# Feeding an adjacency copy into a graph-attention kernel piece by piece, and spreading softmax denominators earlier than they are used

## Chip, cores and metric

One Trainium2 chip, one core. The time is device microseconds of one launch. The kernel before takes 3400.32 us, the median of three runs (3393.2 to 3400.7); the profiled execution spans 3398.4 us. In what follows PE is the matrix engine, DVE the vector engine, ACT the scalar engine, POOL the general engine (it also issues one of the DMA queues), SP the engine that issues the other main DMA queue.

## What is computed

Two graph layers on 4096 nodes with 512 features and one 4096 x 4096 zero/one adjacency. Cut to what matters:

```python
# layer 0: layernorm + relu, then an attention auto-encoder, 4 heads of 128 features
Xw  = einsum('hnd,hde->hne', Xh, W)
sig = sigmoid(f1[:, :, None] + f2[:, None, :])
att = masked_softmax(adj * sig, adj != 0)       # the same att for encoder and decoder
Xa  = einsum('hij,hjd->hid', att, Xw)           # encoder attention
emb = mlp_block(batchnorm(Xa))                  # 512 x 512 product, elu, residual, batchnorm
Y   = einsum('hij,hjd->hid', att, emb)          # decoder attention
out = mlp_block(elu(Y @ W^T));  x = x + out
# layer 1: layernorm + relu, graph attention (GAT), 4 heads of 128
logits = leaky_relu(e_s[:, :, None] + e_n[:, None, :]) + (-1e10) * (1 - adj)
x = x + relu(softmax(logits) @ feats + b)
```

So three attentions of 4 heads x 4096 x 4096 weights each, all float32, with a softmax denominator per target node.

## The kernel before, in words

**Stages.** A first stage normalises x, transposes it and computes the projected features (loop over eight node blocks `ib` of 512, L432-480). Then come encoder attention, an MLP, decoder attention, an MLP, the GAT projection (L695-724) and GAT attention. Features are kept transposed in SBUF: [128 features, 4096 nodes] for each head.

**One attention block.** `attention` (L201) runs eight blocks `n`, one per head `h` and half `tb` of the targets (TB = 2048 targets). A block has 32 steps `j`, each for 128 source nodes. A step loads a mask tile `a` (128 x 2048 bytes, L198, five buffers), makes a weight tile `e` [128, 2048] (encoder and decoder: two ACT passes L400, L401 and the mask multiply on DVE L402; GAT: one ACT pass L761 and one DVE instruction L762) and multiplies it into four PSUM banks with four products of 512 columns (L332, in the profile two records each). The decoder reads every fifth weight tile back from DRAM, where the encoder stored it (`ekeep`).

**Denominators.** They need the sum of all 32 weight tiles over the 128 sources. Each tile goes one of three ways, by the lists ENC_FIRST (encoder blocks 0 and 1), ENC and GAT (L62-64): *moved* tiles are added up in DRAM (`dacc`, L344, a POOL-issued DMA that accumulates, the first of a block only writes; read back at j = 30, L302); *by ones* tiles are multiplied with a matrix of ones on PE (L286); all others are added on DVE into `acc` (L350 the first pair, L352 the rest). At the end PE sums `acc` and the tile read back into the bank `den`.

**Ending of a block.** It is done inside the next block (`ending`, L256), by the list `later` that `at(j, ...)` fills. At step EVICT = 2 ACT copies `den` out (L235), POOL stores it to DRAM (`dens`, L236) and reads it back spread over the partitions (`dcol`, L238); the four output slices are taken out of PSUM. At step 5 DVE inverts (L242, L243) and POOL stores `rinvs` (L244). At steps 6, 9, 12, 15 `spread` (L246) loads slice s of the inverses to all 128 partitions (`rb`, two buffers, L249, POOL queue); at steps 8, 11, 14, 17 DVE scales the slice by it (L491 encoder and decoder, L770 GAT) and two steps later comes the second finishing step (statistics L494, or elu L603, or relu and the output L773, L779).

**What sets the order.** Each engine runs its own list in order. The lists are made by the framework from the program: among the instructions it takes to be ready it prefers the earlier one in the program, so a program position is a preference and not a fixed place. `tc.issue_after(x)` only keeps instructions of x's engine behind x. Everything that POOL issues by DMA (`dacc`, `dens`, `dcol`, `rinvs`, `rb`, the adjacency copy) goes to one DMA queue; mask tiles and x go to SP's; `ekeep` stores to ACT's.

**The adjacency copy.** The input adjacency is float32 in DRAM. Eight DMAs on POOL's queue (L428) copy it as bytes into `masks[t][g]` (t the half of the targets, g a quarter of the sources; 8 MB read and 2 MB written each). Mask tiles are loaded from these. All eight are issued in a row, each made to wait for the last load of x.

Of the kernel before, what the change touches and what calls it, by code (L numbers as in the profile page):

```python
# [41 lines left out]
NIB = N // IB  # L42
# [17 lines left out]


ENC_FIRST = (), (4, 5, 10, 11, 15, 16, 20, 21, 25, 26, 30, 31)  # L62
ENC = (2, 5, 8, 11, 14, 17, 20, 23, 26), (3, 4, 12, 13, 30, 31)
GAT = (1, 3, 6, 8, 11, 13, 16, 18, 21, 23, 26), (14, 30, 31)

KEEP = 5

# [12 lines left out]
def kernel(ctx, tc, x, xT, adjT, w0, w0T, v0, wencT, wdecT, vecs, w1, w1T, a1, outT):  # L80
# [120 lines left out]
    def attention(what, keep, pools, weights, values, row_of, out, finish, ebufs, modes=None, invert=None,  # L201
# [54 lines left out]
        def ending(h, tb, po, den):  # L256

            dcol = denominators(h, tb, den) if den is not None else None
            outs = [out(spool, h, tb, s, po[s]) for s in range(SB)]
            if dcol is not None:  # L260
                at(EVICT + 3, invert_them, h, tb, dcol)
            rbs = {}
            for s, o in enumerate(outs):
                at(EVICT + 4 + 3 * s, lambda s=s: rbs.update({s: spread(h, tb, s)}))
                for k, f in enumerate(finish):
                    at(EVICT + 6 + 3 * s + 2 * k, lambda f=f, s=s, o=o: f(spool, h, tb, s, o, rbs[s], False))

        def next_row_of(h, tb):
            rowb = keep.tile([P, TB], FP, name="rowb", bufs=2)
# [6 lines left out]
        for n, (h, tb) in enumerate(blocks):  # L276
# [15 lines left out]
            for j in range(NJ):  # L292
                for f in later.pop(j, []):
                    f()
                with tc.issue_after(a_load.ins) if j else nullcontext():
                    if (n, j) in extras:
                        extras[n, j]()
                    if not last and j == NJ - 10:
                        next_row = next_row_of(*blocks[n + 1])
                if moved and j == NJ - 2:  # L300
                    back = weight_tile()
                    nc.gpsimd.dma_start(back, dacc[tb])  # L302
                e = weight_tile()
                store = j % KEEP == KEEP - 1 and kept is not None
                if store and kept == "read":
                    a_load = nc.sync.dma_start(e, ekeep[h][tb][j // KEEP])
                else:
                    if masks0:
                        a, a_load = masks0.pop(0)
                    else:  # L310
                        a = mask_tile(keep)
                        a_load = load_mask(a, tb, j)
                    weights(e, rowb, a, j, h, SB if n + j == 0 else 1)
                    if store:
                        stores.append((j // KEEP, e))

                    if j % KEEP == KEEP - 3 and stores:
                        k, t = stores.pop()
                        nc.scalar.dma_start(ekeep[h][tb][k], t)

                def products():
                    nonlocal last_main, last_ones

                    with tc.issue_after(last_ones.ins) if last_ones is not None else nullcontext():

                        if j == EVICT:
                            po.append(bank())
                            for k, t in ahead:
                                nc.tensor.matmul(po[-1], block(values[h], k), t[:, (SB - 1) * IB:SB * IB],
                                                 start=(k == 0), stop=False)  # L330
                        for s, b in enumerate(po):
                            last_main = nc.tensor.matmul(b, block(values[h], j), e[:, s * IB:(s + 1) * IB],  # L332
                                                         start=(j == 0), stop=(j == NJ - 1))
                    last_ones = None


                early = last and j == NJ - 1 and invert is not None
                if not early:
                    products()
                if j < EVICT:  # L340
                    ahead.append((j, e))
                if invert is not None:
                    if j in moved:
                        nc.gpsimd.dma_start(dacc[tb], e, **({"accum_op": ALU.add} if j > moved[0] else {}))  # L344
                    elif j in by_ones:
                        held.append(e)
                    else:
                        adds.append(e)
                        if len(adds) == 2:
                            nc.vector.tensor_add(acc, *adds)  # L350
                        elif len(adds) > 2:
                            nc.vector.tensor_add(acc, acc, e)  # L352

                    if held and j + 1 not in by_ones:
                        with tc.issue_after(last_main.ins):
                            for t in held:
                                add_to_den(t)
# [48 lines left out]
    with tc.tile_pool(name="keep", bufs=1) as keep:  # L406

        with tc.tile_pool(name="f_small", bufs=1) as small, tc.tile_pool(name="f_work", bufs=2) as work:
            xs, loads = [], []
            w0x = small.tile([P, H, DX], FP, name="w0x")  # L410
            v0s = small.tile([P, H, 2], FP, name="v0s")
            nc.scalar.dma_start(v0s, v0)
# [1 line left out]
            for ib in range(NIB):  # L414
                if ib < NIB - 3:
                    xs.append(small.tile([P, C, F], FP, name=f"xs{ib}"))
                else:
                    xs.append((w, *(R[4][:, k * C * F:(k + 1) * C * F].rearrange("p (c f) -> p c f", f=F)
                                    for k in range(2)))[ib - NIB + 3])
                xin = x[ib * IB:(ib + 1) * IB, :].rearrange("(c p) f -> p c f", p=P)  # L420

                for c in range(0, C, 1 if ib == 0 else C):
                    n = 1 if ib == 0 else C
                    loads.append(nc.sync.dma_start(xs[ib][:, c:c + n, :], xin[:, c:c + n, :]))

            for t in range(NTB):
                for g in range(NJ // MG):
                    cast = nc.gpsimd.dma_start(masks[t][g], adjT[g * MG * P:(g + 1) * MG * P, t * TB:(t + 1) * TB])  # L428
                    tc.add_manual_dep(cast.ins, loads[-1].ins.name,
                                      mybir.DependencyInfo(mybir.DependencyClass.Sync, mybir.DependencyReason.DATA),  # L430
                                      reason="features first")
            for ib in range(NIB):  # L432
                st = work.tile([P, C, 6], FP, name="st")
                mv = work.tile([P, C, 2], FP, name="mv")
# [7 lines left out]
                for c in range(C):  # L442
                    by_pool = c == C - 1
                    hn = work.tile([P, F], FP, name="hn", tag="hnp" if by_pool else "hn")
                    (nc.gpsimd if by_pool else nc.vector).tensor_scalar(
                        hn, xs[ib][:, c, :], mv[:, c, 0:1], rstd[:, c:c + 1], ALU.subtract, ALU.mult)
                    pt = bank().rearrange("p (f n) -> p f n", n=P)
                    for fb in range(C):
                        last_pe = nc.tensor.transpose(pt[:, fb, :], hn[:, fb * P:(fb + 1) * P], ident)
                    last_act = nc.scalar.activation(hT[:, :, c * P:(c + 1) * P], pt, AF.Relu)  # L450
# [45 lines left out]
        def encoder_weights():  # L496
            nc.sync.dma_start(w, wencT.rearrange("(c p) o -> p c o", p=P))


# [10 lines left out]
        def three_heads():  # L510
            bn_coefs(stats, "enc_bn_gamma", "enc_bn_beta", a_att, b_att, 0, C - 1)
            add_to_bias(bank(), 0, C - 1, vec_of("enc_mlp_b"))
            for fb in range(C - 1):
                scale_weights(fb)

        with tc.tile_pool(name="enc", bufs=1) as spool:

            with tc.issue_after(last_act.ins), tc.issue_after(masks0[-1][1].ins):
                attention("enc", keep, spool, tanh_weights, R[0:4], lambda h, tb: (rows[tb], h), out_enc,
                          (scaled, statistics), 7, lambda n: ENC if n > 1 else ENC_FIRST, (TINY, ALU.max), "write",  # L520
                          row0=row0, masks0=masks0,
                          extras={(2, 8): encoder_weights, (H * NTB - 1, NJ // 2): three_heads})


        def mlp_block(work, w, src, dst, gamma, beta, scale, between, early=None):
# [255 lines left out]
    with tc.tile_pool(name="gat", bufs=1) as spool:  # L781
        x1_last = []

        def load_last():
# [48 lines left out]
```

## Time and profile before

| stage | us, about | what is busy there |
|---|---|---|
| first stage, and start of encoder block 0 | 0 to 79 | PE, DVE, ACT in turn |
| encoder block 0 | 79 to 209 | ACT 120.5 of 130 |
| encoder block 1 up to the inversion | 209 to 246 | PE 11.1, DVE 9.2, ACT 19.1 of 37 |
| rest of encoder block 1 | 246 to 372 | PE 120.7, ACT 102.9, DVE 116.3 of 126 |
| encoder blocks 2 to 7 | 372 to 1120 | PE 117 to 121, ACT 111 to 119 of 124 or 125 each |
| MLP | 1116 to 1275 | PE 155.1 of 159 |
| decoder attention | 1275 to 2162 | PE 884.5 of 887 |
| MLP's end and GAT projection | 2162 to 2425 | PE 247.5 of 263 |
| GAT attention, 8 blocks | 2425 to 3398 | PE 107 to 124, DVE 100 to 123, of 118 to 130 each |

Read it row by row and not by the page's averages: PE is busy 96% of the span over all, so what can still be won lies in the few places where it is not. The span of a block is the distance between two first denominator additions (L350) on DVE.

### The profile page before, as it was taken

Reading aid. Unit: us, or ns where it says so; the run is one execution under the profiler, and the core shown is the slowest. Engines: PE = TensorE matmul, PEld = TensorE weight load, DVE = VectorE, ACT = ScalarE, POOL = GpSimd, SP = SyncE. Lnnn points to the kernel's source line nnn. Section 1 sums busy time; section 2 is a strip of 40 time slices with the busy share of each in tenths; the row PEclk is TensorE's granted clock in tenths of the full one; section 3 lists DMA queues with packets and bytes.
Section 4 is the critical chain, followed back from the end, with each engine's and each line's share of the span. In section 5 each row is a group of like instructions: output and inputs, shape, how many; then the busy total and the mean of one; then the engine's idle time right before and its main releaser. Section 6 shows DMA issues by size and latency. Waiting matters only on the chain.

```text
span 3398.4 us, 26074 instructions
## 1 busy us (share of the span) xinstructions
PE 3255.4 (96%) x8943; PEld 1501.3 (44%) x8943; DVE 2679.7 (79%) x1912; ACT 2598.4 (76%) x1908; POOL 325.5 (10%) x479
## 2 busy tenths in 40 slices
PE   7969999999999999999999999989999999999999
PEld 6423344344344464444444444448544344444443
DVE  6969799899898775665666556585699999999998
ACT  7969799999999438999999999565665564656553
POOL 2000000010010000000000000024201111111110
PEclk9989999999999999999999999989999999999999
DMA  9994578778777103434444344231388788788876
GB/s 190 195 158 146 163 225 241 205 214 240 208 227 200 55 13 136 142 130 138 145 141 136 133 139 139 62 127 69 94 206 205 186 216 192 196 207 201 208 187 169
DMA packets 180309, 559.60 MB, mean 165 GB/s; under 512 B 20372, under 2 KB 23700, under 8 KB 144208
## 3 DMA queue, kind: packets, MB, share of 16 engines
q0 software_dynamic: 43232, 211.14, 31.7%
q1 hardware_dynamic: 126288, 293.66, 25.8%
q10 hardware_dynamic: 10656, 53.15, 3.9%
q8 instruction: 70, 1.15, 0.1%
q14 instruction: 63, 0.52, 0.0%
HBM read 391.78 MB, written 233.19 MB: 184 GB/s over the span
## 4 chain that ended last, share of the span: by engine, by line
PE 57%; DVE 19%; DMA 11%; issue 9%; ACT 3%; POOL 1%; DVEq 0%; ACTq 0%; POOLq 0%
PE ps L332 42%; DVE e L762 7%; PE ps L533 6%; DMA a<-mask 5%; DVE R L352 5%; DVE e L402 4%; PE ps L707 3%; DMA rb<-rinvs 3%; DMA rinvs<-dcol 1%; PE den L286 1%; DVE acc L352 1%; ACT e L401 1%; ACT e L400 1%; PE ps L467 1%; PE ps L588 1%
## 5 line engine op out<-in xcount | busy, mean ns | idle before, releaser
L332 PE MATMUL ps<-e,R 128*128 128x512 f32 x6048 | 2661.4, 601 | 104.3 <-DVE e L402 70.9
L332 PEld LDWEIGHTS ps<-e,R 128*128 128x128 f32 x6048 | 1155.8, 192 | 1600.2 <-issue 1437.4
L402 DVE TENSOR_TENSOR e<-e,a 128x2048 f32<-128x2048 f32 (+1 forms) x470 | 1050.2, 2259 | 372.5 <-ACT e L401 348.3
L400 ACT ACTIVATE e<-rowb,score 128x2048 f32<-128x2048 f32 (+1 forms) x470 | 913.5, 1968 | 82.4 <-PE ps L332 46.6
L401 ACT ACTIVATE e<-e 128x2048 f32<-128x2048 f32 (+1 forms) x470 | 872.8, 1882 | 44.1 <-DVE e L402 37.6
L761 ACT ACTIVATE e<-rowb,nq,jcol 128x2048 f32<-128x2048 f32 x224 | 454.6, 2085 | 206.9 <-DMA dacc<-e 165.0
L762 DVE SCALAR_TENSOR_TENSOR e<-e,jcol,a 128x2048 f32<-128x2048 f32 (+1 forms) x259 | 589.7, 2316 | 3.8 <-DMA a<-mask 2.6
L352 DVE TENSOR_TENSOR R<-R,e 128x2048 f32<-128x2048 f32 x128 | 291.5, 2278 | 0.0
L352 DVE TENSOR_TENSOR acc<-acc,e 128x2048 f32<-128x2048 f32 x126 | 288.1, 2287 | 2.2
L344 POOL DMA_DIRECT2D dacc<-e x142 | 117.8, 830 | 1087.9 <-DMA dacc<-e 432.7
L533 PE MATMUL ps<-R,w 128*128 128x512 f32 x512 | 220.3, 592 | 0.6 <-DVE w L501 0.6
L249 POOL DMA_DIRECT2D rb<-rinvs x88 | 47.9, 547 | 1135.4 <-DVE R L491 874.5
L533 PEld LDWEIGHTS ps<-R,w 128*128 128x128 f32 x512 | 97.2, 190 | 122.7 <-issue 117.9
L773 ACT ACTIVATE R<-R,vec 128x512 f32<-128x512 f32 x32 | 23.1, 722 | 142.2 <-DVE R L770 141.7
L707 PE MATMUL ps<-w1x,hT 128*128 128x260 f32 x512 | 117.5, 388 | 2.8 <-ACT hT L683 2.8
L553 ACT ACTIVATE ex<-ps,bias 128x512 f32<-128x512 f32 x64 | 44.1, 688 | 97.5 <-PE ps L533 80.4
L707 PEld LDWEIGHTS ps<-w1x,hT 128*128 128x128 f32 x512 | 97.7, 193 | 22.8 <-ACT hT L683 4.4
L286 PE MATMUL den<-e,ones 128*32 128x512 f32 x784 | 93.6, 598 | 0.0
L761 ACT ACTIVATE e<-w,nq,jcol 128x2048 f32<-128x2048 f32 (+1 forms) x35 | 65.6, 1938 | 35.7 <-DMA dacc<-e 32.4
L491 DVE TENSOR_TENSOR R<-R,rb 128x512 f32<-128x512 f32 x60 | 40.5, 686 | 51.6 <-DMA rb<-rinvs 39.4
L555 DVE SCALAR_TENSOR_TENSOR ex<-ex,re 128x512 f32<-128x512 f32 x64 | 45.0, 703 | 36.2 <-ACT re L554 36.1
L712 ACT ACTIVATE R<-ps,rstd 128x128 f32<-128x128 f32 x128 | 38.6, 368 | 39.8 <-PE ps L707 38.9
(154 smaller groups left out, 1209.1 us busy)
## 6 DMA issues: line engine op xcount, KB each, us to landing
a<-mask SPq DMA_DIRECT2D x720, 256.0 KB, 3.3
dacc<-e POOLq DMA_DIRECT2D x142, 1024.0 KB, 8.6
ekeep<-e ACTq DMA_DIRECT2D x48, 1024.0 KB, 9.4
e<-ekeep SPq DMA_DIRECT2D x48, 1024.0 KB, 4.9
rb<-rinvs POOLq DMA_DIRECT2D x88, 256.0 KB, 3.8
mask<-in_adjT POOLq DMA_DIRECT2D x8, 2048.0 KB, 117.6
rowb<-rows SPq DMA_DIRECT2D x16, 1024.0 KB, 6.7
e<-dacc POOLq DMA_DIRECT2D x14, 1024.0 KB, 5.3
```

Of the source, the lines that this page charges most:

```text
L249: nc.gpsimd.dma_start(rb, everywhere(rinvs[h][tb], 0, s * IB, IB))
L286: last_ones = nc.tensor.matmul(den[s * 32:(s + 1) * 32, :], ones[:, 0:32], t[:, s * IB:(s + 1) * IB], start=not begun, stop=stop)
L332: last_main = nc.tensor.matmul(b, block(values[h], j), e[:, s * IB:(s + 1) * IB], start=(j == 0), stop=(j == NJ - 1))
L344: nc.gpsimd.dma_start(dacc[tb], e, **({"accum_op": ALU.add} if j > moved[0] else {}))
L352: nc.vector.tensor_add(acc, acc, e)
L400: nc.scalar.activation(e, rowb, AF.Tanh, bias=column(score[:, 1], j, h), scale=0.5)
L401: nc.scalar.activation(e, e, AF.Exp, scale=0.5)
L402: nc.vector.tensor_mul(e, e, a)
L533: nc.tensor.matmul(z, w[:, fb, o * P:(o + 1) * P], nodes(src[fb], ib), start=(fb == 0), stop=(fb == C - 1))
L707: nc.tensor.matmul(b[:, 0:2 * DX], hT[:, fb, c * P:(c + 1) * P], w1x[:, fb, 2 * k:2 * k + 2, :].rearrange("p h x -> p (h x)"), start=(fb = ...
L761: nc.scalar.activation(e, rowb, AF.Relu, bias=column(nq, j, h), scale=column(jcol, j, h))
L762: nc.vector.scalar_tensor_tensor(e, e, column(jcol2, j, h), a, ALU.add, ALU.mult)
```

## The change

Three edits. The lists ENC and GAT are moved: as many tiles go each way as before (9 moved and 6 by ones; 11 moved and 3 by ones), but the first moved tile is now the block's first, and the others come a step or two earlier (GAT, ENC) or, for by-ones tiles, elsewhere. The ending of a block inverts at step 7 instead of 5, spreads at steps 8, 9, 14, 15 instead of 6, 9, 12, 15, and uses each spread slice five steps after it is issued instead of two; the second finishing step follows one step later instead of two. And the adjacency copy is issued one piece at a time: piece n behind POOL's part of the normalisation of node block n + 1, waiting for the first half of x instead of all of it; the eighth piece is issued in encoder block 1 at step 12. It is for the denominators' DMAs to wait less behind other transfers and for the engines to wait less for them.

```diff
-ENC = (2, 5, 8, 11, 14, 17, 20, 23, 26), (3, 4, 12, 13, 30, 31)
-GAT = (1, 3, 6, 8, 11, 13, 16, 18, 21, 23, 26), (14, 30, 31)
+ENC = (0, 3, 6, 9, 12, 15, 18, 21, 24), (4, 5, 13, 14, 30, 31)
+GAT = (0, 2, 5, 7, 10, 12, 15, 17, 20, 22, 25), (9, 30, 31)
...
-                at(EVICT + 3, invert_them, h, tb, dcol)
+                at(EVICT + 5, invert_them, h, tb, dcol)
             rbs = {}
             for s, o in enumerate(outs):
-                at(EVICT + 4 + 3 * s, lambda s=s: rbs.update({s: spread(h, tb, s)}))
+                j = EVICT + 6 + s % 2 + s // 2 * 6
+                at(j, lambda s=s: rbs.update({s: spread(h, tb, s)}))
                 for k, f in enumerate(finish):
-                    at(EVICT + 6 + 3 * s + 2 * k, lambda f=f, s=s, o=o: f(spool, h, tb, s, o, rbs[s], False))
+                    at(j + 5 + k, lambda f=f, s=s, o=o: f(spool, h, tb, s, o, rbs[s], False))
...
-            for t in range(NTB):
-                for g in range(NJ // MG):
-                    cast = nc.gpsimd.dma_start(masks[t][g], adjT[g * MG * P:(g + 1) * MG * P, t * TB:(t + 1) * TB])
-                    tc.add_manual_dep(cast.ins, loads[-1].ins.name, ...)
+                if ib == NIB // 2 - 1:
+                    half_loaded = load
+            def copy_adjacency(n, behind):
+                t, g = divmod(n, NJ // MG)
+                cast = nc.gpsimd.dma_start(masks[t][g], adjT[g * MG * P:(g + 1) * MG * P, t * TB:(t + 1) * TB])
+                tc.add_manual_dep(cast.ins, behind.ins.name, ...)
...
+                    if by_pool and ib > 0:
+                        with tc.issue_after(made.ins):
+                            copy_adjacency(ib - 1, half_loaded)
...
+                          extras={(1, 12): lambda load: copy_adjacency(7, load),
```

More of the change, by code (lines that the diff above doesn't have):

```diff
@@ L296, in attention @@
                     if (n, j) in extras:
-                        extras[n, j]()
+                        extras[n, j](a_load)
                     if not last and j == NJ - 10:
@@ L408 @@
         with tc.tile_pool(name="f_small", bufs=1) as small, tc.tile_pool(name="f_work", bufs=2) as work:
-            xs, loads = [], []
+            xs = []
             w0x = small.tile([P, H, DX], FP, name="w0x")
@@ L423 @@
                     n = 1 if ib == 0 else C
-                    loads.append(nc.sync.dma_start(xs[ib][:, c:c + n, :], xin[:, c:c + n, :]))
-            for t in range(NTB):
-                for g in range(NJ // MG):
-                    cast = nc.gpsimd.dma_start(masks[t][g], adjT[g * MG * P:(g + 1) * MG * P, t * TB:(t + 1) * TB])
-                    tc.add_manual_dep(cast.ins, loads[-1].ins.name,
-                                      mybir.DependencyInfo(mybir.DependencyClass.Sync, mybir.DependencyReason.DATA),
-                                      reason="features first")
+                    load = nc.sync.dma_start(xs[ib][:, c:c + n, :], xin[:, c:c + n, :])
+                if ib == NIB // 2 - 1:
[3 more added lines that the diff above has]
+                cast = nc.gpsimd.dma_start(masks[t][g], adjT[g * MG * P:(g + 1) * MG * P, t * TB:(t + 1) * TB])
+                tc.add_manual_dep(cast.ins, behind.ins.name,
+                                  mybir.DependencyInfo(mybir.DependencyClass.Sync, mybir.DependencyReason.DATA),
+                                  reason="others first")
             for ib in range(NIB):
@@ L444 @@
                     hn = work.tile([P, F], FP, name="hn", tag="hnp" if by_pool else "hn")
-                    (nc.gpsimd if by_pool else nc.vector).tensor_scalar(
+                    made = (nc.gpsimd if by_pool else nc.vector).tensor_scalar(
                         hn, xs[ib][:, c, :], mv[:, c, 0:1], rstd[:, c:c + 1], ALU.subtract, ALU.mult)
+                    if by_pool and ib > 0:
+                        with tc.issue_after(made.ins):
+                            copy_adjacency(ib - 1, half_loaded)
                     pt = bank().rearrange("p (f n) -> p f n", n=P)
@@ L494, in statistics, with encoder_weights @@
             nc.vector.bn_stats(stats[:, h, tb * SB + s, :], o)
-        def encoder_weights():
+        def encoder_weights(load):
             nc.sync.dma_start(w, wencT.rearrange("(c p) o -> p c o", p=P))
@@ L508, in add_to_bias, with three_heads @@
             nc.vector.tensor_add(bias, pb[:, 0:C], base)
-        def three_heads():
+        def three_heads(load):
             bn_coefs(stats, "enc_bn_gamma", "enc_bn_beta", a_att, b_att, 0, C - 1)
@@ L521 @@
                           row0=row0, masks0=masks0,
[L522 removed]
+                          extras={(1, 12): lambda load: copy_adjacency(7, load),
+                                  (2, 8): encoder_weights, (H * NTB - 1, NJ // 2): three_heads})
         def mlp_block(work, w, src, dst, gamma, beta, scale, between, early=None):
@@ L782, with load_last @@
         x1_last = []
-        def load_last():
+        def load_last(load):
             x1_last.append(spool.tile([P, TB], FP, name="rowb", bufs=2))
```

## The prediction

> **What bounds the kernel now.** I read the page first, then the table of windows by stage, then who waits for whom in the stages where an engine is short of work, then the landing times of single transfers. The windows of encoder block 1's start, an encoder block, the decoder and a GAT block (stretch, length, then busy time of PE, weight loads, DVE, ACT, POOL, PE clock, DMA share, GB/s):
>
> ```profile
> 209.00:246.00 37.00, 11.08 (x32) 4.48 (x24) 9.18 (x8) 19.05 (x11) 1.22 (x2) 0.70 0.97 123
> ...
> 746.00:870.00 124.00, 119.69 (x324) 50.67 (x320) 114.45 (x62) 119.22 (x65) 11.85 (x17) 0.99 0.78 221
> ...
> 1275.00:2162.00 887.00, 884.45 (x2080) 393.48 (x2079) 518.46 (x295) 814.37 (x472) 16.66 (x31) 1.00 0.40 134
> ...
> 2670.00:2790.00 120.00, 115.54 (x294) 49.28 (x293) 112.05 (x56) 69.12 (x41) 17.10 (x23) 0.99 0.83 200
> ```
>
> The decoder is full of matmuls: nothing to win there. Encoder blocks have some 4 us without PE work, GAT blocks 4 to 6, and one place stands empty: 209 to 246. Its waits (engine, line, waited for, total, times, longest):
>
> ```profile
> POOL dcol L238 <- DMA dens<-dsb: 32.8, 1, 32.8
> ...
> PE ps L332 <- DVE e L402: 29.0, 2, 28.7
> DVE dcol L242 <- DMA dcol<-dens: 27.9, 1, 27.9
> ACT e L401 <- DVE e L402: 22.7, 1, 22.7
> ```
>
> The 8 KB store `dens` is issued at 210.79 and lands 33.2 us later, at 244.0, because the eighth adjacency copy, ahead of it on POOL's queue, lands at 243.8 (issued 39.6, landing after 204.2). DVE stands at the inversion with the next weight tile behind it. The copies land in order: 59.3, 84.2, 110.4, 139.9, 169.3, 196.5, 223.8, 243.8, about 26 us each. In the later blocks it is smaller (DVE and PE, encoder block at 745 to 869, then GAT block at 2666 to 2791):
>
> ```profile
> DVE R L491 <- DMA rb<-rinvs: 4.0, 2, 2.9
> ...
> PE ps L332 <- DVE e L402: 4.3, 1, 4.3
> ```
>
> ```profile
> DVE R L770 <- DMA rb<-rinvs: 5.2, 1, 5.2
> DVE dcol L242 <- DMA dcol<-dens: 2.8, 1, 2.8
> ...
> PE ps L332 <- DVE e L762: 4.5, 2, 2.4
> ```
>
> In the encoder block the third `rb` (issued 762.6) lands after 11.2 us, behind the `dacc` issued at 760.8 (11.1 us); the first pair, with nothing before it, took 4.1 to 4.4.
>
> **What the Trainium skill says.** "DMA: Bandwidth & Descriptors", section "Queues, rings and completion order": within a ring descriptors are taken in order, and a DMA engine takes turns between the queues that have work, a packet at a time. The trace agrees with both: `dens` landed 0.2 us after the last copy, while five mask loads on SP's queue beside a copy (issued 59.2 to 61.0, landing after 8.3, 11.4, 14.4, 17.4, 20.5 us) came 3.5 us apart, 262 KB / 3.5 us = 75 GB/s, against 2.6 to 6.7 us each once the copies were over. The same page, "Issuing engines are not separate DMA queues": all queues share the 16 engines, so an earlier copy takes from x. "TensorE: Matmul & The Clock Gate", section "What's actually happening": PE's clock halves after an idle window of about 3.4 us. After the 28.7 us gap 24 matmuls took 13.5 us (563 ns each; 429 at full clock), so a gap costs a little more than its length.
>
> **The change part by part.**
>
> *Copy in pieces.* The same eight DMAs of 0.75 us on POOL; POOL is 10% busy, so the issues cost nothing. In the first stage POOL now finishes its part of block 1 at 19.09 + 2.07 = 21.2, and half of x has landed (the DMAs of the second half land at 23.2, 25.6 and 28.3), so the first piece starts at 21.2 instead of 34.2, 13 us earlier. Seven pieces precede `dens` instead of eight: the seventh landed at 223.8, so now 223.8 - 13 + 3 (shared with x) = 214. `dens` comes at 211 plus the slip below, 214. It then waits 0 to 2 us. DVE was at the inversion at 218.2. So the 27.9 us wait goes, down to 0 to 3. What it is worth on the path: encoder blocks are close to ACT's limit (119.2 of 124), and ACT stood idle 22.7 us, so I count 23, not 28.
>
> *Against it: x.* At 21.2 some 3.8 us x 408 GB/s + 3.3 us x 180 GB/s = 2.1 MB of x are under way (rates from windows of 5 us, the second an estimate between 121 and 408). At the mask loads' 75 GB/s that takes 28 us: the last piece of x lands at about 50 instead of 28.3. Its statistics on DVE began at 43.4 and the last of them ran at 48.8, with hn behind them on DVE and PE's transposes behind those. The slip is 0 (statistics moved behind other work) to 6.6 (50 - 43.4); with a third queue active masks came at 60 GB/s (five in 22 us), which makes 57 and 13.6. I take 3. Copy: 23 - 3 = 20.
>
> *Eighth piece.* Issued about step 8 to 12 of encoder block 1, about 240 to 255, landing by 280. Its first load, for step 24, is issued five steps ahead, at about 209 + 19 x 3.7 = 279, and used at 298: hidden by steps 20 to 23. Behind it on POOL's queue could be the last two `rb`, up to 25 us; they are used at step 19 instead of 14, five steps of 3.7 us more. I take 0, bound 15.
>
> *Longer distance, encoder blocks 2 to 7.* No work is added: the same tiles on the same ways. PE waits for DVE there 7.1, 4.9, 3.9, 4.3, 4.1 and 7.7 us, 32.0 in all, nearly all behind DVE's `rb` waits. The distance helps only where DVE's order follows it. In the block at 746 it does not: the scaling of slices 0 and 1 (program steps 8 and 11) runs after tile 5, as soon as the framework took `rb` to be ready. In its new place the third moved tile is 6, not 5, so slices 2 and 3 no longer sit behind a `dacc`; but tile 3's `dacc` (tile ready at 753.1) now comes right before `rinvs` (753.8). In the block at 375 `rinvs` 0.5 us behind a `dacc` took 8.2 us, against 3.4 in this one. If scaling still comes after tile 5, it waits until 753.8 + 8.2 + 4.3 = 766.3 instead of 761.7, 4.6 us, of which PE, with tile 5 in hand, feels about 2.5; gain 1.8 a block. If it comes after tile 6 or later, all 4.3. I take half of 32: 16.
>
> *GAT.* Here DVE's order follows the program for slices 2 and 3 (after tiles 13 and 16), since DVE always has a tile ready; so five steps, some 17 us, cover `rb` (3.6 to 12). DVE waits over seven block starts: `rb` 4.6 + 5.2 + 3.6 + 1.4 + 6.7 + 1.5 + 1.4 = 24.4; `dcol` 2.8 + 7.0 + 7.1 + 4.3 + 7.1 = 28.3. PE's waits are 2.0 + 4.5 + 6.4 + 4.3 + 1.9 + 2.5 + 4.5 = 26.1. `dcol` waits because `dens` and itself each follow a `dacc`; the new moved tiles, one step earlier, keep that pattern, and two steps later for the inversion help only where it stood at its program place. I remove all of `rb` and a third of `dcol`: 33.8 of 52.7 us, of PE's 26.1 that is 16.7, with the slow clock after gaps 18. The floor is PE: 256 x 0.429 + 5 sums of 0.9 = 114.3 us against 120 to 125 per block.
>
> *Decoder:* its `rb` lie 100 us ahead; all hidden by PE, 884.5 of 887. Zero.
>
> Sum: 20 + 16 + 18 = 54; 3400.3 - 54 = 3346.
>
> **Rivals.**
> - *All waits go.* 23 + 32 + 26 and some 6 of slow clock = 87: 3313. For it: each wait is short and the distance is long. Against: `dens` and `dcol` keep a `dacc` before them.
> - *Only the first stage pays.* DVE's order is made by readiness, so the wait merely moves from `rb` to `rinvs`: 20 to 23 less, 3379.
> - *Slower.* x gives way to the copy (slip 13.6), the last two `rb` wait behind the eighth piece (15), and `rinvs` behind tile 3's `dacc` costs the six encoder blocks 4.6 each (28): 56.6 - 23 = 34 slower, 3434; with half of the encoder's part 3420. For it: 75 GB/s for SP's queue beside a copy is measured. Against: three misfortunes at once.
> - *No change:* the slip and the encoder's loss eat the 23: within 10 us of 3400.
>
> **How the numbers follow.** The forecast gets 0.46, all waits 0.22, first stage only 0.18, slower 0.08, no change 0.06. 3346 is the first. For eight in ten I reach from just below the case of all waits to just above first-stage-only: 3306 to 3388. Faster 0.86, within 0.3% (3390 to 3410) 0.06, slower 0.08.
>
> **What would show it.** The 27.9 us wait at L242 gone, the store `dens` of block 0 landing in under 6 us, the first copy issued near 21 and the seventh landing near 214; the last x load landing near 50; block 1 ending near 350 instead of 369. `rb` waits at L770 at zero, `dcol` waits at L242 still several us in some GAT blocks; PE's waits in encoder blocks halved. Wrong if x lands far later, if L491 waits longer than 4 us a block, or if GAT blocks stay at 120 or above.

## The result, and the profile after

The kernel takes 3363.11 us after the change (median of four runs, 3362.6 to 3364.1) against 3396.76 for the kernel before beside it: a ratio of 0.9904 with a 95% interval of 0.9884 to 0.9924, 33.7 us less. The forecast was 3346, 54 us less, with a range of 3306 to 3388. The time falls inside the range, but the sum under it was not right: one of its three terms, the encoder's, has the wrong sign.

Windows of the changed kernel, in the columns of the windows shown of before (busy time of PE, weight loads, DVE, ACT, POOL, then PE clock, DMA share, GB/s). The rows are the start of encoder block 1, encoder block 5, and two GAT blocks:

```profile
208.00:246.00 38.00, 34.84 (x98) 14.12 (x91) 36.63 (x26) 37.34 (x21) 4.67 (x8) 1.00 0.71 156
722.00:850.00 128.00, 121.83 (x325) 51.38 (x322) 114.46 (x62) 119.60 (x66) 11.88 (x17) 0.97 0.76 214
2764.00:2879.00 115.00, 115.00 (x298) 49.61 (x297) 110.58 (x55) 71.16 (x43) 17.27 (x23) 1.00 0.82 207
2996.00:3118.00 122.00, 117.22 (x299) 49.20 (x298) 113.20 (x57) 71.25 (x43) 17.50 (x24) 1.00 0.82 200
```

First row: PE was busy 11 us of 37 here and is now busy 35 of 38, ACT 37.3 of 38. The hole is gone. Second row: the encoder block has the same ACT and DVE work as before but is 127 us long instead of 124. Last two rows: one GAT block runs at PE's floor (busy 115.0 of 115), and another is 6.5 us longer with 4.8 us of PE idle.

Who waits for whom at the start of block 1 (195 to 260; engine, line, waited for, total, times, longest):

```profile
PE ps L334 <- DVE e L404: 5.4, 4, 2.3
POOL dcol L238 <- DMA dens<-dsb: 4.4, 1, 4.4
...
DVE dcol L242 <- DMA dcol<-dens: 0.7, 1, 0.7
```

The 8 KB store `dens` lands after 4.4 us instead of 33.2, and DVE's wait at the inversion is 0.7 us instead of 27.9. (The line numbers moved: L402 is now L404, L332 is L334, L491 is L500, L762 is L772.)

To see where the 36.7 us between the two profiled spans went, I took the moments at which ACT copies a block's `den` out (L235) as ends of the blocks (for encoder block 7, whose successor belongs to the decoder, the start of ACT's first decoder tile):

| stretch | before, us | after, us | difference |
|---|---|---|---|
| to the end of encoder block 0 | 209.6 | 208.6 | -1.0 |
| encoder block 1 | 159.7 | 129.5 | -30.2 |
| encoder block 2 | 127.4 | 130.4 | +3.0 |
| encoder blocks 3 to 6, each | 124.6 | 127.0 | +9.4 in all |
| encoder block 7 | 127.1 | 132.5 | +5.4 |
| from there to the end of GAT block 0 | 1424.2 | 1425.4 | +1.2 |
| GAT blocks 1 to 6, each | 120.1 | 116.8 | -19.6 in all |
| rest | 131.2 | 126.4 | -4.8 |

So the copy gave 30, the encoder took 18 back, and the GAT gave 24. What the encoder lost is seen in the waits of a block (592 to 716):

```profile
DVE R L500 <- DMA rb<-rinvs: 7.3, 1, 7.3
PE ps L334 <- DVE e L404: 6.7, 4, 4.0
```

DVE waited for `rb` 4.0 us in two pieces in such a block before; now it is 7.3 in one.

The windows over whole stages split each part into PE's idle time and PE's slower running. Encoder block 1: idle 160.0 - 128.7 = 31.3 became 129.0 - 123.6 = 5.4, and busy time fell by 5.2, the clock going from 0.89 to 1.00. GAT from block 1 on: 851.0 - 818.6 = 32.4 idle became 827.0 - 811.1 = 15.9, and busy time fell by 7.5, the clock going from 0.98 to 1.00. That a gap is followed by slow matmuls agrees with the Trainium skill, "TensorE: Matmul & The Clock Gate", section "What's actually happening".

### The profile page after: what moved, and what is told of

The parts are those of the page before. It is cut to its first block, busy times and chain, and to the rows that moved or that the text cites. A ratio compares the mean times of both kernels' runs of the same rounds, so it can differ in the third digit from the quotient of the medians.

```text
span 3361.7 us, 26034 instructions
## 1 busy us (share of the span) xinstructions
PE 3246.9 (97%) x8943; PEld 1495.3 (44%) x8943; DVE 2680.3 (80%) x1912; ACT 2601.9 (77%) x1908; POOL 327.4 (10%) x479
## 5 line engine op out<-in xcount | busy, mean ns | idle before, releaser
L334 PE MATMUL ps<-e,R 128*128 128x512 f32 x6048 | 2651.6, 598 | 77.4 <-DVE e L404 60.4
L334 PEld LDWEIGHTS ps<-e,R 128*128 128x128 f32 x6048 | 1149.2, 191 | 1570.6 <-issue 1420.9
L404 DVE TENSOR_TENSOR e<-e,a 128x2048 f32<-128x2048 f32 (+1 forms) x470 | 1050.6, 2260 | 385.6 <-ACT e L403 363.7
L402 ACT ACTIVATE e<-rowb,score 128x2048 f32<-128x2048 f32 (+1 forms) x470 | 913.3, 1968 | 85.0 <-PE ps L334 47.4
L403 ACT ACTIVATE e<-e 128x2048 f32<-128x2048 f32 (+1 forms) x470 | 872.3, 1881 | 29.9 <-DVE e L404 23.5
L771 ACT ACTIVATE e<-rowb,nq,jcol 128x2048 f32<-128x2048 f32 x224 | 457.9, 2087 | 208.6 <-DMA dacc<-e 132.3
L772 DVE SCALAR_TENSOR_TENSOR e<-e,jcol,a 128x2048 f32<-128x2048 f32 (+1 forms) x259 | 590.6, 2319 | 3.8 <-ACT e L771 3.8
L500 DVE TENSOR_TENSOR R<-R,rb 128x512 f32<-128x512 f32 x60 | 40.5, 685 | 70.7 <-DMA rb<-rinvs 58.6
L771 ACT ACTIVATE e<-w,nq,jcol 128x2048 f32<-128x2048 f32 (+1 forms) x35 | 65.6, 1939 | 32.9 <-DMA dacc<-e 30.2
```

Of the source, the lines that this page charges most:

```text
L402: nc.scalar.activation(e, rowb, AF.Tanh, bias=column(score[:, 1], j, h), scale=0.5)
L403: nc.scalar.activation(e, e, AF.Exp, scale=0.5)
L404: nc.vector.tensor_mul(e, e, a)
L771: nc.scalar.activation(e, rowb, AF.Relu, bias=column(nq, j, h), scale=column(jcol, j, h))
L772: nc.vector.scalar_tensor_tensor(e, e, column(jcol2, j, h), a, ALU.add, ALU.mult)
```

## The experiments

**Theories.** Mine, after seeing the two traces: the three parts of the change are independent; the copy gives about 30 us, the new steps of the ending (the distance) give what the GAT gains, and the new encoder list is what costs. The rivals: the loss in the encoder comes from the new steps and not from the list; the GAT needs the new list for its gain; of the copy, either the earlier start or the later last piece does it alone.

The lengths of the blocks in all kernels (us; the mean of encoder blocks 3 to 6 and of GAT blocks 1 to 6) are the yardstick for what follows:

| kernel | encoder block 1 | encoder 3 to 6 | GAT 1 to 6 | time, us | ratio to before, 95% |
|---|---|---|---|---|---|
| before | 159.7 | 124.6 | 120.1 | 3396.9, 3399.0 | |
| after | 129.5 | 127.0 | 116.8 | 3363.1 | 0.9904 (0.9884 to 0.9924) |
| copy alone | 129.7 | 124.1 | 120.5 | 3368.0 | 0.9916 (0.9899 to 0.9932) |
| lists alone | 158.8 | 126.9 | 120.5 | 3415.5 | 1.0056 (1.0041 to 1.0071) |
| distances alone | 157.6 | 123.9 | 115.0 | 3358.1 | 0.9889 (0.9874 to 0.9904) |
| after, encoder as before | 129.7 | 124.0 | 117.2 | 3343.8 | 0.9847 (0.9832 to 0.9861) |
| after, both lists old | 132.2 | 124.3 | 114.8 | 3330.7 | 0.9797 (0.9782 to 0.9811) |
| after, old GAT list, encoder list with a gap | 128.6 | 121.1 | 114.8 | 3310.4 | 0.9739 (0.9724 to 0.9753) |
| only the last piece later | 141.9 | 123.8 | 120.6 | 3375.5 | 0.9928 (0.9911 to 0.9945) |
| all pieces earlier | 151.8 | 123.8 | 119.8 | 3387.8 | 0.9969 (0.9957 to 0.9981) |

The two times of before are those beside the first four kernels and beside the last four. "After, encoder as before" and the copy alone ran beside 3396.9; both lists old and what stands below it beside 3399.0.

### The copy alone

The changed kernel with the lists and the ending's steps of before:

```diff
-ENC = (0, 3, 6, 9, 12, 15, 18, 21, 24), (4, 5, 13, 14, 30, 31)
-GAT = (0, 2, 5, 7, 10, 12, 15, 17, 20, 22, 25), (9, 30, 31)
+ENC = (2, 5, 8, 11, 14, 17, 20, 23, 26), (3, 4, 12, 13, 30, 31)
+GAT = (1, 3, 6, 8, 11, 13, 16, 18, 21, 23, 26), (14, 30, 31)
...
-                at(EVICT + 5, invert_them, h, tb, dcol)
+                at(EVICT + 3, invert_them, h, tb, dcol)
...
-                j = EVICT + 6 + s % 2 + s // 2 * 6
-                at(j, lambda s=s: rbs.update({s: spread(h, tb, s)}))
+                at(EVICT + 4 + 3 * s, lambda s=s: rbs.update({s: spread(h, tb, s)}))
                 for k, f in enumerate(finish):
-                    at(j + 5 + k, lambda f=f, s=s, o=o: f(spool, h, tb, s, o, rbs[s], False))
+                    at(EVICT + 6 + 3 * s + 2 * k, lambda f=f, s=s, o=o: f(spool, h, tb, s, o, rbs[s], False))
```

> The kernel before with the copy in pieces alone; lists and distances as before. Theory: between before and after, block 0 with the first stage lost 1.1 us and encoder block 1 lost 30.2 us, and both are the copy's doing. So this run is 31 us faster than before (about 3366 if before is 3397), the wait at L242 in encoder block 1 is under 2 us, encoder blocks 2 to 7 take 124 to 127 us each as before and GAT blocks 117 to 123 as before. Rival: part of the 30 us in block 1 comes from the later place of the inversion and of the scaling (steps 7 and 13 instead of 5 and 8); then this run is only some 15 to 23 us faster.

It took 3368.0 us, 28.9 less than before beside it. Block 1 is 129.7 us as in the changed kernel, the other blocks are as before. So the copy's part is 29 us, and none of it depends on the lists or the steps. Its waits at the start of block 1 (195 to 260):

```profile
POOL dcol L238 <- DMA dens<-dsb: 4.4, 1, 4.4
...
DVE dcol L242 <- DMA dcol<-dens: 0.8, 1, 0.8
```

Why 30 in block 1 and not the 23 that the forecast took from ACT's 22.7 us wait? ACT's waits over all of block 1, first of before (195 to 375):

```profile
ACT e L401 <- DVE e L402: 26.8, 2, 22.7
ACT dsb L235 <- PE den L286: 23.5, 2, 13.5
```

and then with the copy alone (195 to 375):

```profile
ACT dsb L235 <- PE den L286: 21.3, 2, 11.2
```

ACT was not short of work only in the 22.7 us. Besides that long wait a second one of 4.1 us for DVE is gone, and its wait for PE's `den` at the end of block 1 is 10.1 us instead of 13.5. (The other wait for `den` in each pair of lines, 10.0 and 11.2 us, is at the end of block 0.) In block 1 ACT thus waited 26.8 + 13.5 = 40.3 us before and 10.1 now: 30.2 less, which is the gain of the block.

### The lists alone

```diff
-ENC = (2, 5, 8, 11, 14, 17, 20, 23, 26), (3, 4, 12, 13, 30, 31)
-GAT = (1, 3, 6, 8, 11, 13, 16, 18, 21, 23, 26), (14, 30, 31)
+ENC = (0, 3, 6, 9, 12, 15, 18, 21, 24), (4, 5, 13, 14, 30, 31)
+GAT = (0, 2, 5, 7, 10, 12, 15, 17, 20, 22, 25), (9, 30, 31)
```

> The kernel before with the new lists ENC and GAT alone. Theory: with tile 3 moved, its accumulating transfer of 1 MB stands in front of the store of the inverses in every encoder block from 2 on, while DVE's order is the same as before; so encoder blocks 2 to 7 are 18 us slower in all, DVE waits about 7 us a block at the scaling, and GAT hardly changes (0 to 8 us faster): 10 to 18 us slower than before, about 3410. Rival: the encoder's loss comes from the new distances; then this run is within 5 us of before or faster.

It took 3415.5, 18.6 us more than before. The encoder blocks 3 to 6 are 126.9 us, as long as in the changed kernel, and DVE's wait is the same to the tenth (623 to 750):

```profile
DVE R L491 <- DMA rb<-rinvs: 7.3, 1, 7.3
PE ps L332 <- DVE e L402: 6.8, 4, 4.0
```

The loss in the encoder is the list's. The GAT's list, with the steps of before, leaves the blocks at 120.5, though not for want of an effect: over the seven GAT block starts DVE's `rb` waits come to 17.6 us instead of 24.4, and its `dcol` waits to 36.7 instead of 28.3.

### The distances alone

```diff
-                at(EVICT + 3, invert_them, h, tb, dcol)
+                at(EVICT + 5, invert_them, h, tb, dcol)
             rbs = {}
             for s, o in enumerate(outs):
-                at(EVICT + 4 + 3 * s, lambda s=s: rbs.update({s: spread(h, tb, s)}))
+                j = EVICT + 6 + s % 2 + s // 2 * 6
+                at(j, lambda s=s: rbs.update({s: spread(h, tb, s)}))
                 for k, f in enumerate(finish):
-                    at(EVICT + 6 + 3 * s + 2 * k, lambda f=f, s=s, o=o: f(spool, h, tb, s, o, rbs[s], False))
+                    at(j + 5 + k, lambda f=f, s=s, o=o: f(spool, h, tb, s, o, rbs[s], False))
```

> The kernel before with the new steps of inversion, spreading and scaling alone, lists and copy as before. Theory: in the encoder DVE's order does not follow the program place (slices 0 and 1 are still scaled after tile 5), so encoder blocks keep 124 to 127 us; in GAT it does, and GAT's 24 us are this edit's: about 3373, waits for rb at L780 zero, waits for dcol at L242 still 4 to 7 us in the later GAT blocks. Rival: GAT's gain is the new list's; then this run is within 5 us of before.

It took 3358.1, 38.8 us less, more than I expected of it, and 5 us less than the whole change. In the encoder the distance does next to nothing (123.9 a block instead of 124.6): in blocks 3 to 7 DVE's order is the same as before, inversion after tile 3, two slices scaled after tile 5 and two after tile 7, although the program places the work up to five steps later. In the GAT it takes the blocks to 115.0, and there is no PE wait left to speak of (window of a block, and DVE's and PE's waits in it, 2999 to 3114):

```profile
2999.00:3114.00 115.00, 115.00 (x298) 49.73 (x297) 113.30 (x57) 70.33 (x42) 17.14 (x23) 1.00 0.88 213
```

```profile
DVE R L772 <- DMA rb<-rinvs: 1.7, 1, 1.7
...
PEld ps L334 <- DVE e L764: 0.5, 2, 0.2
```

There DVE's order did follow: in before the slices were scaled after tiles 8, 10, 13, 16 or 10, 10, 13, 16 (in one block 9, 10, 13, 16), here after 12, 13, 18, 19. DVE's `dcol` waits, which I had expected at 4 to 7 us in the later GAT blocks, are 2.7 to 5.4 us in four of them and gone in the others: 17.0 in all.

### The change with the encoder's list and steps of before

```diff
-ENC = (0, 3, 6, 9, 12, 15, 18, 21, 24), (4, 5, 13, 14, 30, 31)
+ENC = (2, 5, 8, 11, 14, 17, 20, 23, 26), (3, 4, 12, 13, 30, 31)
...
-                at(EVICT + 5, invert_them, h, tb, dcol)
+                at(EVICT + (3 if what == "enc" else 5), invert_them, h, tb, dcol)
...
-                j = EVICT + 6 + s % 2 + s // 2 * 6
+                j = EVICT + 4 + 3 * s if what == "enc" else EVICT + 6 + s % 2 + s // 2 * 6
...
-                    at(j + 5 + k, lambda f=f, s=s, o=o: f(spool, h, tb, s, o, rbs[s], False))
+                    at(j + (2 + 2 * k if what == "enc" else 5 + k), lambda f=f, s=s, o=o: f(spool, h, tb, s, o, rbs[s], False))
```

> The changed kernel with the encoder's list and the encoder's steps put back; copy in pieces, GAT's list and steps as changed. Theory: the encoder's 18 us come back and nothing else moves: 3363 - 18 = 3345, encoder blocks 2 to 7 at 124 to 127 us. Rival: the encoder is slower after because block 1 ends earlier or the transfers of the copy run into it; then this run stays within 5 us of 3363.

It took 3343.8, 19.3 us less than the changed kernel, and its encoder blocks are 124.0 again. The encoder's part of the change is thus a loss of 18 to 19 us, whatever else is there. But its GAT blocks, at 117.2, do not reach the 115.0 of the distances alone; what differs in the GAT is its list, which the next kernel puts back.

### The change without its lists

```diff
-ENC = (0, 3, 6, 9, 12, 15, 18, 21, 24), (4, 5, 13, 14, 30, 31)
-GAT = (0, 2, 5, 7, 10, 12, 15, 17, 20, 22, 25), (9, 30, 31)
+ENC = (2, 5, 8, 11, 14, 17, 20, 23, 26), (3, 4, 12, 13, 30, 31)
+GAT = (1, 3, 6, 8, 11, 13, 16, 18, 21, 23, 26), (14, 30, 31)
```

> The changed kernel with both lists put back: copy in pieces and the new distances together. Theory: the two edits touch different stretches (first stage and block 1; GAT), so they add: 29 + 39 = 68 us faster than before, about 3329, GAT blocks 1 to 6 at 114 to 117 us. Rival: after the copy, GAT or encoder blocks change for another reason and the sum doesn't hold; then 3340 or more.

It took 3330.7. The copy alone gave 28.9 and the distances alone 38.8; 67.7 together, and this kernel is 68.4 below before: the two parts add. Its GAT blocks are 114.8 each, the last four of the six to the tenth. It is 13 us below the kernel of the section before, which also has the encoder's old steps; in the profiles this one comes to the end of GAT block 0 4.8 us later and takes 16.5 less from there. Against the changed kernel, which differs in the lists alone, it takes 14.4 us less from there. So the new GAT list costs some 14 to 16 us once the distance is there, while it cost nothing without it.

How it costs is seen where POOL issues the denominators. In the changed kernel, at the start of GAT block 5, ACT copied `den` out from 2996.35 to 2996.9. POOL's timeline (start, us, what is issued, and in brackets the idle time before it and who ended it):

```profile
2995.38 0.88 POOL L346 DMA_DIRECT2D dacc<-e  x1 [4.71 <-DMA dacc<-e]
3004.03 0.86 POOL L346 DMA_DIRECT2D dacc<-e  x1 [7.78 <-DMA dacc<-e]
3012.52 0.85 POOL L346 DMA_DIRECT2D dacc<-e  x1 [7.63 <-DVE e L772]
3013.06 0.87 POOL L236 DMA_DIRECT2D dens<-dsb  x1
3021.50 0.59 POOL L238 DMA_DIRECT2D dcol<-dens  x1 [7.57 <-DMA dens<-dsb]
```

`dens` could go at 2996.9 and goes at 3013.1, 16 us later. It stands in POOL's list behind two accumulations that are not ready: the first waits at the head of the list until the accumulation before it has landed, the second, by the profile, for its weight tile (the accumulation before it had landed only 0.5 us earlier). Then it lands 8.1 us later, behind the one just issued. In the kernel with the distances alone, where `den` was copied out from 2999.4 to 3000.0:

```profile
3000.96 0.87 POOL L346 DMA_DIRECT2D dacc<-e  x1 [4.95 <-DMA dacc<-e]
3001.52 0.87 POOL L236 DMA_DIRECT2D dens<-dsb  x1
3009.62 0.58 POOL L238 DMA_DIRECT2D dcol<-dens  x1 [7.23 <-DMA dens<-dsb]
```

Here `dens` goes 1.5 us after `den` is there. What DVE and PE feel in the changed kernel's block (2996 to 3118):

```profile
DVE dcol L242 <- DMA dcol<-dens: 8.8, 1, 8.8
...
PE ps L334 <- DVE e L772: 4.8, 6, 1.4
```

Over seven GAT block starts DVE's `dcol` waits come to 28.3 us before, 30.1 in the changed kernel, and 14.6 in this one without its lists; its `rb` waits to 24.4, 1.4 and 1.2; PE's waits for DVE's weight tiles to 26.1, 9.8 and none.

### A list with a gap at the start

If the encoder's loss comes from an accumulation standing ahead of `rinvs` on POOL's queue, a list in which no moved tile falls between the first and the sixth should give the wait back, and with the new steps also what the old list lost. As many tiles go each way as before; the GAT's list is the old one.

```diff
-ENC = (0, 3, 6, 9, 12, 15, 18, 21, 24), (4, 5, 13, 14, 30, 31)
-GAT = (0, 2, 5, 7, 10, 12, 15, 17, 20, 22, 25), (9, 30, 31)
+ENC = (0, 6, 9, 12, 15, 18, 21, 24, 26), (3, 4, 13, 14, 30, 31)
+GAT = (1, 3, 6, 8, 11, 13, 16, 18, 21, 23, 26), (14, 30, 31)
```

> As e5, with an encoder list whose second moved tile is 6 and by-ones tiles 3 and 4 instead of 4 and 5: (0, 6, 9, 12, 15, 18, 21, 24, 26), (3, 4, 13, 14, 30, 31). On POOL's queue no accumulating transfer now stands between dens and the fourth rb. Theory: the encoder's waits come from transfers of 1 MB ahead of rinvs or rb on that queue and from nothing else, so DVE's waits at the scaling fall under 1.5 us a block, encoder blocks 2 to 7 come to about 120 us (ACT's 119.2 and a little) and the kernel to about 3329 - 22 = 3307. Rival: with the waits gone, ACT's wait for the bank den or DVE's additions set the block, which stays at 123 or above; then 3325 or more.

It took 3310.4, a ratio of 0.9739, 88.6 us below before and 53 below the changed kernel: faster than both. First the changed kernel in the encoder block at 722, POOL's timeline and then DVE's:

```profile
723.97 0.58 POOL L236 DMA_DIRECT2D dens<-dsb  x1 [7.20 <-issue]
725.93 0.57 POOL L238 DMA_DIRECT2D dcol<-dens  x1 [1.38 <-DMA dens<-dsb]
729.57 0.88 POOL L346 DMA_DIRECT2D dacc<-e  x1 [3.06 <-DVE e L404]
732.13 0.57 POOL L244 DMA_DIRECT2D rinvs<-dcol  x1 [1.68 <-DVE dcol L243]
738.92 1.08 POOL L249 DMA_DIRECT2D rb<-rinvs  x2 [6.22 <-DMA rinvs<-dcol]
```

```profile
732.16 4.49 DVE L404 TENSOR_TENSOR e<-e,a 128x2048 f32<-128x2048 f32 x2 [0.32 <-ACT e L403]
744.47 0.69 DVE L500 TENSOR_TENSOR R<-R,rb 128x512 f32<-128x512 f32 x1 [7.82 <-DMA rb<-rinvs]
```

`rinvs` is issued 2.6 us behind a `dacc` that lands after 8.9 us, and lands with it, after 6.5; the first `rb` then takes 5.5, and DVE, free at 736.6, stands until 744.5. The Trainium skill, "DMA: Bandwidth & Descriptors", section "Queues, rings and completion order", says that the descriptors of a ring are taken in order, and promises no order of completion; that the small transfer lands with the large one ahead of it is what this trace shows. Before, `rinvs` stood 2.6 us behind a `dacc` too:

```profile
751.26 0.54 POOL L344 DMA_DIRECT2D dacc<-e  x1 [0.84 <-DVE e L402]
753.83 0.55 POOL L244 DMA_DIRECT2D rinvs<-dcol  x1 [2.04 <-DVE dcol L243]
```

But that one was the block's first, which only writes: it landed after 5.2 us and `rinvs` after 3.4. In encoder blocks 3 to 7 the `dacc` ahead of `rinvs` takes 5.0 to 5.2 us before and 7.6 to 9.1 in the changed kernel. The new list did not put a large transfer where there was none; it put an accumulating one, which takes longer, where one stood that only writes. With the gap, the block at 702:

```profile
703.56 0.58 POOL L236 DMA_DIRECT2D dens<-dsb  x1 [5.75 <-issue]
705.51 0.58 POOL L238 DMA_DIRECT2D dcol<-dens  x1 [1.37 <-DMA dens<-dsb]
711.72 0.55 POOL L244 DMA_DIRECT2D rinvs<-dcol  x1 [5.63 <-DVE dcol L243]
713.69 1.08 POOL L249 DMA_DIRECT2D rb<-rinvs  x2 [1.42 <-DMA rinvs<-dcol]
719.46 1.14 POOL L249 DMA_DIRECT2D rb<-rinvs  x2 [4.69 <-DVE R L500]
722.27 0.90 POOL L346 DMA_DIRECT2D dacc<-e  x1 [1.67 <-DVE e L404]
```

`rinvs`, with nothing ahead of it, lands after 1.7 us. From `rinvs` to `rb` it is 2.0 us instead of 6.8, both pairs of `rb` go out, and only then comes the accumulation. No wait of DVE for `rb` is left; what is left in a block (590 to 710) is the other way round, DVE waiting for ACT:

```profile
DVE e L404 <- ACT e L403: 5.9, 6, 2.8
...
PE ps L334 <- DVE e L404: 2.4, 2, 1.8
```

and the block is ACT's (its encoder block at 702 and GAT block at 2837):

```profile
702.00:823.00 121.00, 118.45 (x321) 49.82 (x321) 114.64 (x62) 119.17 (x65) 11.83 (x17) 1.00 0.80 226
2837.00:2952.00 115.00, 115.00 (x298) 49.55 (x297) 110.81 (x55) 70.87 (x43) 17.14 (x23) 1.00 0.84 207
```

ACT is busy 119.2 of 121, PE 115.0 of 115 in the GAT. This kernel also puts the by-ones tiles 4 and 5 at 3 and 4 again, and the moved tile after 24 at 26; the run doesn't separate these from the gap, but the waits that went are those of `rb`.

### The copy taken apart

First the kernel before with only its last piece issued later; the other seven go in a row behind all of x, as before:

```diff
-            for t in range(NTB):
-                for g in range(NJ // MG):
-                    cast = nc.gpsimd.dma_start(masks[t][g], adjT[g * MG * P:(g + 1) * MG * P, t * TB:(t + 1) * TB])
...
+            for n in range(7):
+                copy_adjacency(n, load)
...
+                          extras={(1, 12): lambda load: copy_adjacency(7, load),
```

> The kernel before with the eighth piece of the copy alone moved to encoder block 1, the other seven in a row behind all of x as before. Theory: the seventh piece then lands near 224 as before, dens (ready near 210) behind it, the inversion is reached at 218 and waits some 8 us: about 20 us faster than before. Rival: the earlier start is what pays; then only 10 us or less.

It took 3375.5, 23.5 us less, somewhat more than the 20 expected. Then all eight pieces inside the first stage, the last one right behind the seventh:

```diff
                     if by_pool and ib > 0:
                         with tc.issue_after(made.ins):
                             copy_adjacency(ib - 1, half_loaded)
+                            if ib == NIB - 1:
+                                copy_adjacency(7, half_loaded)
...
-                          extras={(1, 12): lambda load: copy_adjacency(7, load),
```

(against the copy alone).

> The kernel before with the copy in pieces during the first stage, the eighth behind the seventh there instead of in block 1. Theory: the eighth piece then lands near 233 (the changed kernel's seventh at 212.5 and 20 to 27 more), and the inversion waits some 15 us: 12 to 16 us faster than before; together with e7 the two halves explain the 29 to 31 of the copy. Rival: the last piece's place is all that counts; then no gain over before.

It took 3387.8, 11.2 us less, a little short of the 12 to 16 expected. DVE's wait at the inversion, with only the last piece later:

```profile
DVE dcol L242 <- DMA dcol<-dens: 10.0, 1, 10.0
```

and with all pieces earlier, where I had expected some 15:

```profile
DVE dcol L242 <- DMA dcol<-dens: 19.5, 1, 19.5
```

Neither half does it alone. Together with before and the copy alone they make a scale: waits of 27.9, 19.5, 10.0 and 0.8 us go with block lengths of 159.7, 151.8, 141.9 and 129.7. From end to end that is 30.0 us of block for 27.1 of wait, so each microsecond of this wait costs a little over one of time, and DVE's wait is the better measure of the gain than ACT's longest. The later last piece takes 18 us out of the wait, the earlier start 8; the forecast said 13 for the start.

## Why the prediction was right or wrong

**Copy, forecast 20 less: about 30 less.** The mechanism was right: the store waited behind the last copy; it lands after 4.4 us now, and DVE's wait is gone. Two terms were mis-sized. The 23 was ACT's longest wait alone; with the copy alone ACT's waits in block 1 fell by 30.2, and in PE's view of the changed kernel the block won 25.8 us of idle time and 5.2 of slow matmuls. The forecast had noted that a gap costs more than its length, and then took less than the gap's length. The other term, 3 us for the slip of x, measured nothing: the end of block 0 comes 1.0 us earlier. The first copy was issued at 20.3 (21.2 forecast) and the last load of x came in sooner than forecast. The loads of x and then the copies in the changed kernel (how long from issue to landing):

```profile
L426 SPq DMA_DIRECT2D R<-in_x x2: 2707/4067/5427, 8.8 to 14.3; - x2
...
DMA to landing us min/median/max: 3.6/9.8/26.2
```

```profile
L432 POOL DMA_DIRECT2D mask<-in_adjT x8: 776/812/977, 20.3 to 233.2; - x8
...
DMA to landing us min/median/max: 27.8/76.6/157.4
```

The last x load, issued at 14.3, landed 26.2 us later, at 40.5, not at 50. It was not the rate that was off but the amount. Two windows of the changed kernel (the last column, GB/s, is of all queues together):

```profile
20.00:25.00 5.00, 4.65 (x34) 4.16 (x33) 4.05 (x18) 3.97 (x15) 1.24 (x2) 1.00 1.06 391
25.00:30.00 5.00, 5.00 (x42) 4.50 (x40) 4.84 (x19) 4.45 (x20) 2.88 (x2) 1.00 1.06 164
```

The forecast let the copy share from its issue on, with 2.1 MB of x under way. But the copy's first packet moved only at 24.5, 4.2 us after its issue; until then x kept its full rate (409 GB/s from 20 to 24.5 us, by the packets of SP's queue), and 0.8 MB was left. Then x got 80 GB/s from 25 to 31, near the 75 of the forecast, and 24 after that. DVE's statistics waited for no load of x after the first 12 us. The longest copy, 157.4 us after its issue at 55.1, is the seventh: 212.5 (214 forecast).

**Eighth piece, forecast 0: 0.** It was issued at 233.2 and landed 30.1 us later at 263.3, and nobody waited for it.

**Encoder blocks 2 to 7, forecast 16 less: 18 more.** This is the step that failed. The forecast described the case that came: if the scaling still comes after tile 5, it waits behind the third tile's `dacc` and `rinvs`. It did, in all of blocks 3 to 7. (Before, `rinvs` stood behind a `dacc` as well, but behind one that only writes; see the list with a gap.) The fault is in the sizes put on it. The 4.6 us was how much later the scaling would come, and the forecast set the 2.5 us that PE was to feel of it against the 4.3 that PE had waited, as if those all went away. In the block at 722, set against the one at 746 of before and measured from ACT's copy of `den`, the scaling begins 22.2 us later instead of 15.5, so 6.7 later: `rinvs` is issued 2.2 us later, since tile 0 is a moved one now, so that DVE's first addition (of tiles 1 and 2, not 0 and 1) no longer fills its wait for ACT at the block's start but stands right ahead of the inversion; it lands 3.1 us more slowly behind the accumulating `dacc` (6.5 for 3.4); and `rb` takes 1.4 more. Before, DVE had waited 1.1 us at this place and 2.9 at the third `rb`; the second went, the first became 1.1 + 6.7 = 7.8. PE, with tile 5 in hand, felt 4.5 of it at one place, not 2.5. Over the six blocks PE's idle time went from 31.9 to 46.5 us and its busy time from 721.2 to 724.3; together these are the 17.7 us. The prediction named "L491 waits longer than 4 us a block" as a sign that it was wrong, and that sign showed: 6.8 to 10.3 us a block.

**GAT, forecast 18 less: 24.4 less.** The `rb` waits went as forecast, 24.4 to 1.4. A third of the `dcol` waits was to go too; they stayed, 30.1 for 28.3. What failed is the sentence that "the new moved tiles, one step earlier, keep that pattern", which put the list's own cost at nothing: with the old list the distance halves these waits (14.6), and the new list brings them back. PE's idle time fell by 16.5, near the 16.7 of the forecast, but PE's busy time fell by 7.5 for the better clock, where the forecast counted some 1.3. So the GAT came near by two errors with opposite signs.

**Decoder, forecast 0:** from the encoder's end to the end of GAT block 0 the time differs by 1.2 us.

The sum is -30.2 + 17.7 - 24.4 - 1.0 + 1.2 = -36.7, the time between the profiled spans. That the total lies inside the range is in part luck: the encoder missed its forecast by 34 us, and the copy and the GAT, mis-sized the other way, made good 17 of them. Of the rivals, "only the first stage pays" had the encoder's mechanism right, "the wait merely moves from `rb` to `rinvs`", but not the GAT. "All waits go", 3313, is what the list with a gap reaches at 3310: the waits could be had, and it was the lists that kept them. They cost about 32 us: with both old lists the profile is 17.6 us shorter up to the end of GAT block 0 and 14.4 shorter after it, and the same change gives 68 us.

## What to carry to other kernels

Where small transfers that someone waits for share a queue with large ones, count who stands ahead of each small one at the moment when it is ready, both in the queue (the large one's remaining time is added) and in the issuing engine's list (a large one that is not ready yet holds up all behind it); moving the large ones a step or two can lose as much as moving the waits wins. A longer distance in the program pays only where the engine's order follows the program, so look up between which instructions the work really stands before counting on it. And when a delay is worked out, add it to the wait that is there already instead of comparing it with it.

## What the hardware showed that was not expected

- A gap in PE's work cost more than the gap: 25.8 us of idle time less in encoder block 1 brought 5.2 us of faster matmuls with it, 16.5 us less in the GAT brought 7.5, though PE's waits for DVE there were only 1.9 to 6.4 us a block before.
- A copy issued while another queue is busy did not take from it at once: its first packet moved 4.2 us after its issue, and the loads of x fell from 409 GB/s to 80 only then.
- Of the 1 MB transfers into `dacc` of the changed kernel, the 14 that only write (each block's first) landed after 4.7 to 6.4 us, the 128 that accumulate after 7.6 to 13.5. The 8 KB `rinvs` took 5.4 to 6.8 us behind an accumulating one in encoder blocks 3 to 7, and 1.7 with nothing ahead.
